# One kernel, one change: the four gating products of an adapter column block put in one row with priority

## The chip, the cores and the metric

The kernel runs on one core of one Trainium2 chip. The metric is the device time of one execution in microseconds (us); of several executions the median is used. A profile is one execution recorded by the hardware profiler; its times are counted from the first instruction of the program.

The engines have short names in the profile: PE is TensorE (matmuls; PEld its weight loads), DVE is VectorE, ACT is ScalarE, POOL is GpSimd, SP is SyncE, which here only issues DMAs. A q after the name means the engine's instruction queue.

## What is computed

Two batches of 1024 rows and 2048 columns pass through two steps, both with a layer norm in front and a residual sum behind. Cut to what matters:

```python
x = x + matmul(fake_quant(layernorm(x), s1, z1), fake_quant(ctx_4096, s2, z2))
u = layernorm(x)                       # seen as 8 groups of 256 rows
A_eff = einsum('bn,nri->bri', gate, lora_A)     # 16 adapters of rank 32, 8 groups
B_eff = einsum('bn,nor->bor', gate, lora_B)
delta = einsum('bor,btr->bto', B_eff, einsum('bri,bti->btr', A_eff, u))
delta += einsum('or,btr->bto', lora_B_shared, einsum('ri,bti->btr', lora_A_shared, u))
x = x + matmul(u, kernel) + bias + delta
```

The change concerns `A_eff` and `B_eff`: for each group the 16 adapters are summed with the group's gates as weights. The kernel does these sums on TensorE, as products with a small gate matrix.

## The kernel before

**Stages.** Each batch has a quantised stage (the first matmul, in bf16) and then a feed-forward stage (the second matmul in f32, by seven outer times seven inner products of half blocks, `product` at L813 and L829, which takes the place of eight by eight). The profile shows the quantised stage of batch 0 in the first 178 us and that of batch 1 from about 550 to 713 us.

**Pairs.** In the quantised stage the unit of work is a pair (`Pair`, L513): one block of 512 columns `n` and one group `g` of 256 rows. Its accumulator `pa` has two halves of 128 rows, one bank each. For each half, ACT first writes a starting value into the bank (`begin`, L526, which reads a row term and the column term of the block), and then 16 bf16 products of 128x128 by 128x512 are added on PE (L530). When both halves are done, DVE adds the pair to `y` (`end`, L547) and takes statistics (L551). Three accumulators go round, so that the pair after the next but one waits for `end`. `begin` is queued with priority (L558).

**Adapters.** For each of four column blocks of `lora_A` and of `lora_B`, and for each batch, `gated_sums` (L570) computes one tile `pg` of 128 rows and 512 columns: four products with the gate matrix `gmat` (128x32) as weights, each of which writes its own 32 rows of `pg`. That makes 16 calls with 64 products; an f32 product stands in the trace as two matmul records, so there are 128 records. The four inputs come in two loads of two parts; SP issues each part as a DMA (L216) into buffers named `lit`, of which there are ten. After two products the buffer of the first load is given back and the next load is traced (`load_next`, L204), then the same for the second load. `gated_copy` (L588, L591) has DVE copy `pg` into one of three buffers `q2b`, which the quantisation of the context uses in turn as well. For `lora_A` four transposes `pga` (L601) and four small copies (L607) follow; for `lora_B` eight DMAs to `bd` in device memory (L617).

**Buffers in PSUM.** `pg` comes from the pool `ps_m` under the tag `pm`, which has two buffers. The same two serve `pt` (L423, transposes of the quantised rows), `pcp` and `pc` (L486 and L505, column sums of the context block), `pga`, `ptz` (L633, transposes of the second norm) and `px` (L649).

**What sets the order.** The instructions are traced in program order, and a planner at compile time lays out each engine's queue from that trace: whenever an engine is free in the planner's own model of the run, it takes the ready instruction with the lowest priority number, which is its place in the trace. Ready means that what it depends on is done and that a buffer of its tag is free. Inside `tc.high_priority()` the numbers are those of the start of the program. On the chip each engine then works through its queue strictly in that order and waits on semaphores. The first 78 us or so and part of what follows are an exception: the steps of `entry` (L923) are chained by hand (`STEPS`, `in_order`), the calls for column blocks 0 and 1 of `lora_A` in batch 0 among them (steps g0 and g1). The other 14 calls are free: `lora_a_step` (L594, called at L1049 and L1063) and `lora_b_step` (L612, called at L1066 and L1084), all between pairs.

Of the kernel before, what the change touches and what calls it, by code (L numbers as in the profile page):

```python
# [98 lines left out]
def tile_quant_xattn_then_lora_ffn(  # L99
# [33 lines left out]
    GP = GPB * RC  # L133
# [70 lines left out]
    def load_next():  # L204
        while todo and len(loaded) < ahead[0] and todo[0][0] <= batch[0] and lit.spare:
            _, srcs = todo.popleft()
            if isinstance(srcs, int):
                load_x(0, srcs)
                continue
            buf = lit.take()  # L210
            t = flat(buf).rearrange("p (k n) -> p k n", k=2)
            if len(srcs) == 1:
                nc.sync.dma_start(out=t, in_=srcs[0])
            else:
                for c, src in enumerate(srcs):
                    nc.sync.dma_start(out=t[:, c, :], in_=src)  # L216
            loaded.append((len(srcs), buf, t))

    def next_loaded(parts):

        got = next(e for e in loaded if e[0] == parts)
        loaded.remove(got)
        return got[1:]
# [342 lines left out]
    def gated(nm):  # L566

        return gated_copy(gated_sums(nm))

    def gated_sums(nm):  # L570
        ps = ps_m.tile([P, NB], F32, tag="pm", name=f"pg_{nm}")
        for h in range(2):
            buf, t = next_loaded(2)
            for c in range(2):
                row = (2 * h + c) * GP
                nc.tensor.matmul(  # L576
                    ps[row : row + GP, :],
                    gmat.rearrange("p i a r -> p (i a r)"),
                    t[:, c, :],
                    start=True,  # L580
                    stop=True,
                    skip_group_check=True,
                )
            lit.give(buf)
            load_next()
        return ps
# [336 lines left out]
    def entry():  # L923
# [21 lines left out]
        def ad_sums(n):  # L945
            ad[n] = gated_sums(f"a0_{n}")
# [275 lines left out]
```

## Time and profile before

| | us |
|---|---|
| median of 3 runs | 1090.87 |
| the three runs | 1091.78, 1090.87, 1089.13 |
| the profiled execution, first to last instruction (its span) | 1086.6 |
| PE busy | 1063.4 (98% of the span) |
| DVE busy | 759.3 (70%) |
| ACT busy | 247.6 (23%) |
| POOL busy | 267.8 (25%) |
| DMA traffic | 261.35 MB, 241 GB/s in the mean |
| granted TensorE clock, mean | 0.994 |

The profile gives no other time of its own for the profiled execution than the span. The timed runs lie 4.3 us above it in the median, for what comes before the first and after the last instruction. A difference of about 0.3% (3.3 us) is what a measurement of this kernel can tell from none.

How to read the lines that follow in this document: a line of a timeline gives the start and the length of a run of like instructions on one engine, then the engine, the line of the code, what is written and read with the tile shape, and how many instructions there are. Brackets at the end give the idle time of the engine before it and what ended it. A run of matmuls ends when its last matmul has left the array; the next run can start before that, since matmuls overlap.

### The profile page before, as it was taken

How to read it: one execution, taken by the hardware profiler on the slowest of the kernel's cores; microseconds unless marked ns; L12 is line 12 of the kernel's file. 1: busy time of each engine (PE TensorE's matmuls, PEld its weight loads, DVE VectorE, ACT ScalarE, POOL GpSimd, SP SyncE). 2: the span in 40 equal slices, each digit the busy share in tenths (PEclk: the TensorE clock that was granted, in tenths of full speed). 3: DMA queues.
4: the chain of work that ended last, by engine and by line, in shares of the span. 5: the costliest groups of instructions: out<-in, count | busy, mean ns of one | idle time of the engine just before them, and what ended most of it. 6: DMA issues, size and time to landing. Idle time of an engine off the chain costs nothing.

```text
span 1086.6 us, 10640 instructions
## 1 busy us (share of the span) xinstructions
PE 1063.4 (98%) x3932; PEld 491.3 (45%) x3932; DVE 759.3 (70%) x941; ACT 247.6 (23%) x351; POOL 267.8 (25%) x112
## 2 busy tenths in 40 slices
PE   5999999999999999999999999999999999999998
PEld 2444445544444444444444433555444444444443
DVE  7986776756877686677858645757569677756851
ACT  5866133210000000001676631331000000000000
POOL 0000003243434314362000000034344532253500
PEclk7999999999999999999999999999999999999999
DMA  9979758876897575798682394679668874748511
GB/s 344 378 200 295 214 189 327 311 250 218 290 361 271 181 269 182 255 357 300 221 281 49 124 245 164 222 273 349 237 237 292 293 266 154 270 144 301 212 40 58
DMA packets 120380, 261.35 MB, mean 241 GB/s; under 512 B 11400, under 2 KB 15624, under 8 KB 119304
## 3 DMA queue, kind: packets, MB, share of 16 engines
q1 hardware_dynamic: 99840, 219.24, 59.1%
q10 hardware_dynamic: 20168, 40.38, 10.9%
q0 software_dynamic: 320, 1.05, 0.3%
q8 instruction: 31, 0.51, 0.2%
q14 instruction: 21, 0.17, 0.1%
HBM read 224.99 MB, written 37.75 MB: 242 GB/s over the span
## 4 chain that ended last, share of the span: by engine, by line
PE 87%; DVE 5%; DMA 4%; ACT 2%; issue 1%; SPq 0%; ACTq 0%
PE fu L829 34%; PE fv L829 17%; PE pa L530 14%; PE fw L829 9%; DMA lit<-in_ctx_dram 3%; PE pl L695 3%; PE px L649 3%; PE ptz L633 2%; DMA y<-in_x_dram 1%; PE pg_b L576 1%; DVE st L383 1%; PE pg_a L576 1%; ACT big L412 1%; PE pt L423 1%; DVE big L629 1%
## 5 line engine op out<-in xcount | busy, mean ns | idle before, releaser
L829 PE MATMUL fu<-big,lit 128*128 128x512 f32 x896 | 395.3, 593 | 0.0
L829 PEld LDWEIGHTS fu<-big,lit 128*128 128x128 f32 x896 | 168.7, 190 | 206.2 <-issue 204.9
L530 PE MATMUL pa<-big,big 128*128 128x512 bf16 x1024 | 238.8, 381 | 5.0 <-DVE big L428 2.6
L829 PE MATMUL fv<-big,lit 128*128 128x512 f32 x448 | 197.9, 594 | 0.0
L772 POOL TENSOR_TENSOR lit<-lit,lit 128x1024 f32<-128x1024 f32 x56 | 164.2, 2940 | 116.4 <-PE fw L829 49.2
L763 POOL TENSOR_TENSOR lit<-lit,lit 128x1024 f32<-128x1024 f32 x40 | 100.2, 2508 | 289.1 <-DMA lit<-zs 257.7
L772 DVE TENSOR_TENSOR big<-big,big 128x2048 f32<-128x2048 f32 x56 | 159.6, 2853 | 5.9 <-PE ptz L633 5.3
L530 PEld LDWEIGHTS <-big 128*128 128x128 bf16 x1024 | 96.7, 98 | 136.5 <-issue 31.8
L853 DVE TENSOR_TENSOR y<-y,fu 128x1024 f32<-128x1024 f32 x92 | 108.6, 1215 | 50.7 <-PE fu L829 50.5
L829 PEld LDWEIGHTS fv<-big,lit 128*128 128x128 f32 x448 | 84.3, 190 | 105.0 <-issue 104.7
L853 DVE TENSOR_TENSOR y<-y,fv 128x1024 f32<-128x1024 f32 x48 | 56.8, 1218 | 89.4 <-PE fv L829 89.4
L458 ACT ACTIVATE q2b<-lit,sc,inv 128x1024 int16<-128x1024 f32 x64 | 76.3, 1232 | 161.8 <-DMA lit<-in_ctx_dram 126.1
L763 DVE TENSOR_TENSOR big<-big,big 128x2048 f32<-128x2048 f32 x40 | 104.2, 2604 | 11.8 <-DMA big<-in_w_dram 11.8
L829 PE MATMUL fw<-big,lit 128*128 128x512 f32 x224 | 99.6, 593 | 0.0
L680 POOL DMA_DIRECT2D bp<-bd x4 | 2.7, 664 | 376.8 <-DVE rstd_z L358 183.4
L684 ACT COPY pl<-bias 128x1024 f32<-128x1024 f32 x16 | 16.3, 1018 | 294.4 <-DVE y L706 281.4
L547 DVE SCALAR_TENSOR_TENSOR y<-pa,k_s,y 128x1024 f32<-128x1024 f32 x32 | 41.0, 1280 | 47.0 <-PE pa L530 46.8
L829 PEld LDWEIGHTS fw<-big,lit 128*128 128x128 f32 x224 | 41.8, 190 | 51.4 <-issue 50.2
L853 DVE TENSOR_TENSOR y<-y,fw 128x1024 f32<-128x1024 f32 x24 | 28.4, 1216 | 50.9 <-PE fw L829 50.9
L526 ACT ACTIVATE pa<-bp,r_s 128x512 f32<-128x512 f32 x58 | 39.0, 685 | 84.8 <-PE pa L530 54.8
L383 DVE BATCH_NORM_STATS2 st<-y 128x6 f32<-128x512 f32 x64 | 41.4, 680 | 5.4 <-DMA y<-in_x_dram 5.3
L551 DVE BATCH_NORM_STATS2 st<-y 128x6 f32<-128x512 f32 x64 | 40.1, 678 | 0.1
(92 smaller groups left out, 637.3 us busy)
## 6 DMA issues: line engine op xcount, KB each, us to landing
big<-in_w_dram SPq DMA_DIRECT2D x96, 1024.0 KB
lit<-zs SPq DMA_DIRECT2D x88, 512.0 KB
lit<-in_ctx_dram SPq DMA_DIRECT2D x64, 512.0 KB
out_dram<-y ACTq DMA_DIRECT2D x30, 512.0 KB
zs<-lit ACTq DMA_DIRECT2D x24, 512.0 KB
lit<-in_lora_a_dram SPq DMA_DIRECT2D x32, 256.0 KB
lit<-in_lora_bt_dram SPq DMA_DIRECT2D x32, 256.0 KB
y<-in_x_dram SPq DMA_DIRECT2D x16, 512.0 KB
```

Source lines behind the costliest of these rows:

```text
L383: nc.vector.bn_stats(st1[:, self.m, n, :], self.y[:, ds(n * NB, NB)])
L458: nc.scalar.activation(qi, t, AF.Relu, bias=z2, scale=inv2)
L526: nc.scalar.activation(self.pa[:, j, :], colt[self.n], AF.Identity, bias=r_s[:, m : m + 1])
L530: nc.tensor.matmul(self.pa[:, j, :], self.c1T[:, k, ds(j * P, P)], self.c2[k // 8][:, k % 8, :], start=not self.begun[j], stop=(k == KT - ...
L547: return nc.vector.scalar_tensor_tensor(yp, self.pa, s12, yp, ALU.mult, ALU.add)
L551: nc.vector.bn_stats(st2[:, self.g * MG + j, self.n, :], y[self.g][:, j, ds(self.n * NB, NB)])
L649: nc.tensor.matmul(px[i * 2 * R : (i + 1) * 2 * R, :], acat[:, k, ds(3 * pr + i, 2), :].rearrange("p s r -> p (s r)"), zqs[i][k // KQ][:, ...
L695: nc.tensor.matmul(pl[j][i][:, half], axT[rows, pr, ds(j * P, P)], bt[rows, half], start=False, stop=True, skip_group_check=True,)
L763: line(eng.tensor_tensor(got[0], got[0], got[1], ALU.add if terms[1][2] > 0 else ALU.subtract))
L772: line(eng.tensor_tensor(out_t, at[p], at[q], op))
L829: nc.tensor.matmul(ps[m], at[:, k, ds(m * P, P)], bt[:, k, :], start=(opens and k == 0), stop=(ends and k == KQ - 1), skip_group_check=True,)
L853: line(nc.vector.tensor_tensor(yp, yp, whole[chain], op))
```

## The change

`gated_sums` takes both loads first. The four products are then issued in one block, inside `tc.high_priority()`, and from the last row block to the first. Both buffers are given back, and the next loads traced, after all four.

```diff
     def gated_sums(nm):
         ps = ps_m.tile([P, NB], F32, tag="pm", name=f"pg_{nm}")
-        for h in range(2):
-            buf, t = next_loaded(2)
-            for c in range(2):
-                row = (2 * h + c) * GP
+        got = [next_loaded(2) for _ in range(2)]
+        with tc.high_priority():
+            for c in (3, 2, 1, 0):
                 nc.tensor.matmul(
-                    ps[row : row + GP, :],
+                    ps[c * GP : (c + 1) * GP, :],
                     gmat.rearrange("p i a r -> p (i a r)"),
-                    t[:, c, :],
+                    got[c // 2][1][:, c % 2, :],
                     start=True,
                     stop=True,
                     skip_group_check=True,
                 )
+        for buf, _ in got:
             lit.give(buf)
             load_next()
         return ps
```

The shapes, the number of products, their inputs and the copies behind them stay as they are.

## The prediction

> **What bounds the kernel.** I read the page first, then the PE timeline around every call of the gating products, then who waits for whom.
>
> ```profile
> span 1086.6 us, 10640 instructions
> ...
> PE 1063.4 (98%) x3932; PEld 491.3 (45%) x3932; DVE 759.3 (70%) x941; ACT 247.6 (23%) x351; POOL 267.8 (25%) x112
> ...
> PE 87%; DVE 5%; DMA 4%; ACT 2%; issue 1%; SPq 0%; ACTq 0%
> ```
>
> PE is busy 98% of the span and makes 87% of the chain that ended last. In the two stretches with gating products (80 to 160 us, 605 to 695 us) PE is busy in nearly every microsecond, so PE time taken out there should reach the end, unless something else then comes late.
>
> The timeline of PE shows how the 16 calls stand now. One call is a whole row of four products (8 records), another is broken:
>
> ```profile
> 79.25 1.02 PE L530 MATMUL pa<-big,big 128*128 128x512 bf16 x4 [0.43 <-ACT pa L526]
> 80.20 1.06 PE L576 MATMUL pg_a<-lit,gmat 128*32 128x512 f32 x8
> 81.20 1.47 PE L530 MATMUL pa<-big,big 128*128 128x512 bf16 x6
> ```
>
> ```profile
> 99.74 5.13 PE L530 MATMUL pa<-big,big 128*128 128x512 bf16 x23
> 104.80 1.05 PE L576 MATMUL pg_a<-lit,gmat 128*32 128x512 f32 x2
> 105.78 3.63 PE L530 MATMUL pa<-big,big 128*128 128x512 bf16 x16
> 109.34 1.06 PE L576 MATMUL pg_a<-lit,gmat 128*32 128x512 f32 x6
> 110.33 5.86 PE L530 MATMUL pa<-big,big 128*128 128x512 bf16 x26
> ```
>
> The reader is to see that two records, six and eight all take 1.05 or 1.06 us: products that write different rows of `pg` run side by side in the array, and each group pays once, however many stand in it. Seven calls are whole (they start at 80.20, 83.03, 119.15, 128.24, 158.63, 617.04 and 693.06 us). Nine are broken into one product, then 16 products of a pair, then three (104.80, 132.79, 141.88, 608.82, 636.92, 646.44, 657.90, 666.99 and 676.07 us; the three follow 4.5 us later).
>
> **What a group costs.** Take it from the starts of its neighbours. Sixteen `pa` products take 3.63 us and the last lasts 0.38, so they follow each other at (3.63 - 0.38) / 15 = 0.216 us. The last `pa` before the lone product started at 99.74 + 5.13 - 0.38 = 104.49; the next starts at 105.78. Without the group it would have come 0.216 after the former, so the lone product costs 105.78 - 104.49 - 0.216 = 1.07 us. The three cost 110.33 - 109.03 - 0.216 = 1.08 us. The row of four costs 81.20 - 79.89 - 0.216 = 1.09 us. A broken call pays 1.07 + 1.08 = 2.15, a whole one 1.09: **1.06 us less for each of nine calls, 9.6 us in all.** That would be the answer if the place of the lone product cost nothing otherwise.
>
> **The cover that goes.** All nine lone products stand between the two halves of a pair. There PE has something to wait for:
>
> ```profile
> 616.51 0.60 PE L601 MATMUL pga<-ident,q2b 128*128 128x128 f32 x4
> 617.04 1.06 PE L576 MATMUL pg_a<-lit,gmat 128*32 128x512 f32 x8
> 618.04 1.47 PE L530 MATMUL pa<-big,big 128*128 128x512 bf16 x6
> 620.29 0.38 PE L530 MATMUL pa<-big,big 128*128 128x512 bf16 x1 [0.78 <-ACT pa L526]
> ```
>
> ```profile
> L526 ACT ACTIVATE pa<-bp,r_s x30: 670/691/692, 559.6 to 697.1; 128x512 f32<-128x512 f32 x30
> ...
> its engine sat idle before it (us, times) until:
>   PE pa L530: 32.6, 9
> ```
>
> The starting value of a second half (L526, 0.69 us) waits for the last product of the first half, though it writes another bank; ACT's idle time in that stretch ends on `pa` nine times. At 620.29 nothing filled the hole: from product to product PE needed 1.159 us in place of 0.216, so an open hand-over loses 0.94 us. The lone product covers just this hole. If all four move elsewhere, the hole needs another cover. The first products of the next pair can be it, where that pair's first half has its starting value: at 114.7, 569.5, 576.5 and 593.8 us they are, and the step across the hand-over is only 0.295 to 0.297 us, a loss of 0.08. At 631.4 us it is 0.464, a loss of 0.25.
>
> So a call whose row falls into the hand-over saves 1.06 us; a call whose row falls elsewhere saves 2.15 - 1.09 - 0.08 = 0.98 with the next pair as cover, and 2.15 - 1.09 - 0.94 = 0.12 with an open hand-over. Ends for the nine: 1.1 and 9.6 us. I take 0.98 for eight and 0.12 for one, the call at 657.90: there the next pair needs a new column term, which DVE only ends at 658.6 us (L511 begins at 657.79 and takes 0.81), so its products can't stand in. 8 x 0.98 + 0.12 = **8.0 us**. The mean loss over the six uncovered hand-overs above, 0.25 us, would give 9 x (1.06 - 0.25) = 7.3, which is close.
>
> **Where the rows go.** With priority they go when their four parts have landed and one of the two `pm` buffers is free, and before any `pa` product. Landing: DMA is saturated from 84 to 122 us (its share is 1.00 to 1.08 in most stretches of 4 us) and idle at 124 to 128, so every adapter load of batch 0 is in by about 122. The loads of `lora_B` are 16 DMAs of 256 KB issued from 104.3 to 115.2; at some 274 GB/s one takes 0.96 us; counted back from 122, my estimate is 110, 114, 118 and 122 us for the four blocks, against starts at 128.2, 132.8, 141.9 and 158.6. In batch 1 DMA stays full until about 647, and the same count gives 625 to 628 us for the block that starts at 636.9. Most rows can come earlier by several us, without a wait for data.
>
> **The other parts.** The next loads are traced after all four products, not after two. In a whole row the products start 7 ns apart, so that delay is nothing; in a broken call the second product came with the last group anyway. SP's own waits for `pg_a` are 9.5 us in three cases, all with DMA work still queued; an earlier row only shortens them. Taking both loads first needs two buffers that are already loaded: no instruction. DVE has the same 16 copies of 0.68 us, and between 104 and 120 us it is busy without a break, so an early row waits for its copy with a `pm` buffer in hand: nothing if the second buffer suffices, priced below if not. The order 3, 2, 1, 0 changes no cost, as each product writes its own rows. The feed-forward stages keep every instruction; the chains through DVE at their start (PE waits there at 184.2 and 719.1 us) begin at the end of a pair and move with it.
>
> The Trainium skill has a rule that speaks against the row: "TensorE: Matmul & The Clock Gate", Part 3, says that a weight load overlaps products in flight only when it goes to another row group. Here the four products share all rows and differ in columns. By that rule six further weight loads of 0.108 us each (the median of the trace) would stand in line, a row would cost 1.09 + 0.65 = 1.74 us, and the change would save 9 x (2.15 - 1.74) = 3.7 us before the hand-overs. The trace shows otherwise: the row of four at 80.20 has its first four weight loads 5 to 7 ns apart and costs 1.09 us.
>
> **The sum.** The span is 1086.6, and 1086.6 - 8.0 = 1078.6. The timed runs lie 4.3 us above the span, so the forecast for the median is 1090.87 - 8.0 = **1082.9 us**.
>
> **Rivals.**
> 1. The cover is missed: most hand-overs stay open, because the next pair isn't ready in the planner's order. Nine times 0.12 saves 1.1 us: 1089.8. For it: 620.29. Against it: four of six uncovered hand-overs lost only 0.08.
> 2. Rows queued before their loads land. The planner's picture of DMA time may be too short where DMA is saturated, and PE's queue is strict. The exposed blocks are the third and fourth of `lora_A` and perhaps two of `lora_B` in each batch. A row queued right after the column sums of batch 1 (about 625 us) meets data at 625 to 628, so 0 to 3 us; I take 4 us over both batches: 1086.9. Against it: now PE ends a wait on adapter data once, 0.4 us.
> 3. It doesn't do what it says: with priority the two products of the first load go as soon as they are ready, and the others later. A call then still pays twice, and whole calls break. No gain: 1090.9.
> 4. **Slower:** early rows hold the `pm` buffers. A row takes a buffer when its data are there but gives it back only after its copy, which keeps its place on DVE and needs a `q2b` buffer. In batch 1 the first block of `lora_A` is loaded by about 550 us and its copy stands at 614.8; a row that went at 550 would keep one of two buffers for 60 us. Transposes (`pt`, eight tiles from 583 to 608 us), column sums and `ptz` (32 tiles) would go through one buffer, each waiting for the copy of the one before: 0.68 us (L428) and its hand-offs, about 0.9. It decides from 8.0 / 0.9, nine such waits that nothing fills; with some 16 of them the result is 1090.9 - 8.0 + 14.4 = 1097.3. Against it: PE has products of pairs to put into most of these waits.
>
> **Chances.** The forecast (within about 2 us) 0.60; rival 2, 0.10; rival 1, 0.10; rival 3, 0.05; rival 4, 0.15. About 0.3% (3.3 us) is what a measurement of this kernel can tell from no change. Forecast and rival 2 lie below 1087.6: faster 0.70. Rivals 1 and 3: same 0.15. Rival 4: slower 0.15. The range leaves rival 4 out. Its low end is the full 9.6 us and the spread of the runs, 1.3 us: 1080.0. Its high end takes in rivals 1 to 3 with the spread: 1092.2.
>
> **What would show it.** Right: the PE timeline has 16 groups of eight records at L576, none of two or six; each costs 1.09 us by its neighbours; steps across the old hand-overs are about 0.3 us; the end of the quantised stage comes about 3 us earlier in batch 0 and 5 us in batch 1. The sum would be wrong if hand-overs at L530 show idle time that ends on ACT L526 (rival 1), if L576 waits for DMA (rival 2), if groups of two and four records appear (rival 3), or if `pt`, `ptz`, `pcp` or `pc` wait for DVE copies with `pg` in between (rival 4).

## The result, and the profile after

The changed kernel takes 1106.92 us (median of 4 runs, 1104.97 to 1107.41) against 1091.01 for the kernel before on the same chip: a ratio of 1.0164, 95% interval 1.0146 to 1.0181. It is slower: the medians are 15.9 us apart, the ratio makes it some 18 us. The forecast was 8 us faster, and the time lies above the range. (The experiments ran on other chips, where the kernel before took 1087.3 to 1088.7 us. They are compared by ratio to the kernel before on their own chip.)

First the page of the changed kernel, the same lines that were read before:

```profile
span 1105.6 us, 10625 instructions
...
PE 1062.2 (96%) x3932; PEld 493.7 (45%) x3932; DVE 757.2 (68%) x941; ACT 247.4 (22%) x351; POOL 262.1 (24%) x112
...
PE 79%; DMA 10%; DVE 7%; ACT 2%; issue 1%; SPq 0%; ACTq 0%; DVEq 0%
```

The span grew by 19.0 us, while PE busy fell by only 1.2. PE idle time (span less busy) went from 23.2 to 43.4 us. In the chain that ended last, DMA rose from 4 to 10%. So PE now waits, and more of the chain that ended last is transfers.

The rows themselves are as forecast. The PE timeline has all 16 calls whole, and two calls of a batch even stand as one group:

```profile
128.31 1.06 PE L575 MATMUL pg_b<-lit,gmat 128*32 128x512 f32 x8
129.31 0.39 PE L530 MATMUL pa<-big,big 128*128 128x512 bf16 x1
129.63 1.92 PE L575 MATMUL pg_b<-lit,gmat 128*32 128x512 f32 x16
```

The time went at the start of both feed-forward stages. The first outer product there (`fu`) is followed by `fw`, which needs the weight block b21: SP loads it in two DMAs of 1 MB (L753), and DVE adds the two (L763). In the timeline of the changed kernel, batch 0 and then batch 1:

```profile
185.76 3.60 PE L829 MATMUL fu<-big,lit 128*128 128x512 f32 x8
192.76 2.29 DVE L763 TENSOR_TENSOR big<-big,big 128x2048 f32<-128x2048 f32 x1 [7.56 <-DMA big<-in_w_dram]
195.11 6.47 PE L829 MATMUL fw<-big,lit 128*128 128x512 f32 x10 [5.75 <-DVE big L763]
...
728.54 4.45 DVE L763 TENSOR_TENSOR big<-big,big 128x2048 f32<-128x2048 f32 x1 [8.06 <-DMA big<-in_w_dram]
733.05 1.12 PE L829 MATMUL fw<-big,lit 128*128 128x512 f32 x2 [3.27 <-DVE big L763]
738.76 1.94 PE L633 MATMUL ptz<-ident,big 128*128 128x128 f32 x8 [4.59 <-DVE big L629]
```

Read the brackets from the bottom up: PE waits for DVE, DVE waits for the load. In batch 1 the norm of the next tile (L629) stands behind the late sum in DVE's queue, and there is a second wait of 4.59 us. The three waits are 13.6 us.

In batch 0 the load explains the wait: the sum takes its usual 2.29 us. In batch 1 it takes 4.45, and two small steps of the norm (L349) take 4.40 us together, where they take 0.35 in batch 0. POOL's own sums (L772) stand beside them:

```profile
728.50 2.34 POOL L772 TENSOR_TENSOR lit<-lit,lit 128x1024 f32<-128x1024 f32 x1 [9.16 <-DMA zs<-lit]
730.92 4.27 POOL L772 TENSOR_TENSOR lit<-lit,lit 128x1024 f32<-128x1024 f32 x1
733.10 4.40 DVE L349 SCALAR_TENSOR_TENSOR nt_z<-ve_z,r_z 128x1 f32<-128x1 f32 x2
735.15 2.33 POOL L772 TENSOR_TENSOR lit<-lit,lit 128x1024 f32<-128x1024 f32 x1
```

The DVE sum ends at 732.99, 2.15 us after the end of the first POOL sum; the two small steps end at 735.21 and 737.51, each 0.02 us after the end of a further one. So DVE stood still while POOL's sums ran. All 20 traces of this case agree: each of the 673 sums of weight blocks on DVE that took more than 2.32 us ended 2.14 to 2.16 us after the end of a POOL sum that it met, and each of the 20 steps at L349 that took more than 0.4 us ended 0.01 to 0.02 us after one. Of the 7.86 us of waiting in batch 1, an estimate from these durations, (4.45 - 2.29) + (4.40 - 0.35) = 6.2 us, is POOL's hold on DVE. The load is still behind it in part: POOL's sums had waited for DMA too (9.16 us for `zs`), so all came at once.

In the kernel before, PE did not wait there. But look how close it was, in its timeline (the lines of POOL are the sums that ran when b21 landed):

```profile
183.60 2.70 POOL L772 TENSOR_TENSOR lit<-lit,lit 128x1024 f32<-128x1024 f32 x1
185.13 3.60 PE L829 MATMUL fu<-big,lit 128*128 128x512 f32 x8
186.07 2.38 DVE L763 TENSOR_TENSOR big<-big,big 128x2048 f32<-128x2048 f32 x1 [1.50 <-DMA big<-in_w_dram]
188.57 4.50 PE L829 MATMUL fw<-big,lit 128*128 128x512 f32 x10
...
718.43 2.69 POOL L772 TENSOR_TENSOR lit<-lit,lit 128x1024 f32<-128x1024 f32 x1
720.54 2.74 DVE L763 TENSOR_TENSOR big<-big,big 128x2048 f32<-128x2048 f32 x1 [1.15 <-DMA big<-in_w_dram]
723.40 4.50 PE L829 MATMUL fw<-big,lit 128*128 128x512 f32 x10
```

The sum ends at 186.07 + 2.38 = 188.45, and `fw` starts at 188.57; in batch 1 it is 723.28 and 723.40. **Block b21 was ready 0.12 us ahead of its use, in both batches, and DVE had idled for its data before that.** The 0.12 itself comes from POOL, whose sums end 2.15 us ahead of those on DVE here too (186.30 and 721.13). With the usual 2.29 us the block would have been ready at 188.36 and 722.83, an estimate that leaves the load 0.2 and 0.6 us to spare. So the kernel before was bound there by PE and, within 0.6 us, by a chain through DMA as well.

A long wait is paid twice. Ten `fw` records took 4.50 us before and take 6.47 after the wait. The stretches of the changed kernel around it say why; behind the busy times stand the granted clock, the DMA share and GB/s:

```profile
185.00:190.00 5.00, 4.36 (x16) 2.10 (x15) 0.20 (x3) 1.37 (x4) 4.52 (x2) 1.00 1.00 384
190.00:195.00 5.00, 0.00 (x0) 0.00 (x0) 2.24 (x2) 0.00 (x0) 0.00 (x0) 0.72 0.65 261
195.00:200.00 5.00, 4.89 (x7) 2.21 (x8) 2.41 (x11) 0.00 (x0) 0.00 (x0) 0.60 0.72 261
```

After the idle stretch the granted clock is 0.60. The Trainium skill ("TensorE: Matmul & The Clock Gate", Part 1) says that the array falls to half its clock after about 3.4 us without work and stays there until it has been busy for as long. The trace agrees in kind, with a granted clock of 0.50 from 192.2 to 198.9 us and 6.47 us for 4.50 us of work. But the clock fell sooner, 2.8 us after PE's last matmul (189.36), and waits of 1.9 to 2.8 us brought a lower clock at times as well (last section).

The sum: idle time +20.2 us. PE busy -1.2, of which the rows take away some 8 (measured below as 8.1), so that other matmuls were busy some 7 us longer. The low clock accounts for about 5 of these, by an estimate: PE was busy for 10.1 us in the stretches with a clock of 0.50 (192.2 to 198.9, 635.9 to 639.3 and 734.9 to 741.7 us), and half of that is extra. Together 19.0.

**Why is b21 late?** Look at SP's timeline, of the kernel before and then of the changed one. The bd DMAs (L617) carry a copied `pg` to device memory, eight per call of `lora_B`; the loads at L753 are weight blocks:

```profile
126.61 2.10 SPq L753 DMA_DIRECT2D big<-in_w_dram  x2
130.25 5.24 SPq L617 DMA_DIRECT2D bd<-q2b  x8
137.43 0.93 SPq L753 DMA_DIRECT2D big<-in_w_dram  x2
```

```profile
130.24 5.07 SPq L617 DMA_DIRECT2D bd<-q2b  x8
135.41 6.44 SPq L753 DMA_DIRECT2D big<-in_w_dram  x3
141.94 1.21 SPq L617 DMA_DIRECT2D bd<-q2b  x2
...
178.98 1.67 SPq L753 DMA_DIRECT2D big<-in_w_dram  x2
```

The early row let the planner queue the eight bd DMAs of the first call ahead of the first weight loads. On the chip they wait for the copy (L591) until 130.24, so SP does nothing for 12 us and DMA is idle from 125 to 130 us (share 0.01; 0.39 before). In the kernel before, SP stood still for 10.9 us there, until a pair gave the weight block its buffer (L530, 126.6), and its first bd DMAs started at the same 130.25. The first weight block now starts 8.8 us later. Not all of that is SP's order: with the loads first (below) they start at 131.29, when a buffer comes free. The loads of b21 start at 178.98 and 179.48, where they started at 173.56 and 178.54.

### The profile page after: what moved, and what is told of

Same layout as the page of the kernel before. It is cut to its first block, busy times and chain, and to the rows that moved or that the text cites. A ratio compares the mean times of both kernels' runs of the same rounds, so it can differ in the third digit from the quotient of the medians.

```text
span 1105.6 us, 10625 instructions
## 1 busy us (share of the span) xinstructions
PE 1062.2 (96%) x3932; PEld 493.7 (45%) x3932; DVE 757.2 (68%) x941; ACT 247.4 (22%) x351; POOL 262.1 (24%) x112
## 4 chain that ended last, share of the span: by engine, by line
PE 79%; DMA 10%; DVE 7%; ACT 2%; issue 1%; SPq 0%; ACTq 0%; DVEq 0%
PE fu L829 33%; PE fv L829 17%; PE pa L530 10%; PE fw L829 9%; DMA big<-in_w_dram 4%; PE pl L695 3%; PE px L649 2%; PE ptz L633 2%; DMA y<-in_x_dram 2%; DVE st L383 1%; DMA lit<-in_lora_a_dram 1%; DMA gate_b<-in_gate_dram 1%; DVE big L763 1%; DMA lit<-in_ctx_dram 1%; DMA bd<-q2b 1%
## 5 line engine op out<-in xcount | busy, mean ns | idle before, releaser
L530 PE MATMUL pa<-big,big 128*128 128x512 bf16 x1024 | 238.1, 383 | 6.3 <-DVE big L428 2.5
L772 POOL TENSOR_TENSOR lit<-lit,lit 128x1024 f32<-128x1024 f32 x56 | 161.3, 2889 | 151.8 <-PE fw L829 77.8
L763 POOL TENSOR_TENSOR lit<-lit,lit 128x1024 f32<-128x1024 f32 x40 | 96.9, 2423 | 295.2 <-DMA lit<-zs 258.6
L772 DVE TENSOR_TENSOR big<-big,big 128x2048 f32<-128x2048 f32 x56 | 158.0, 2824 | 5.1 <-PE ptz L633 4.6
L530 PEld LDWEIGHTS <-big 128*128 128x128 bf16 x1024 | 98.0, 98 | 133.9 <-issue 26.3
L763 DVE TENSOR_TENSOR big<-big,big 128x2048 f32<-128x2048 f32 x40 | 105.7, 2642 | 27.8 <-DMA big<-in_w_dram 27.8
L829 PE MATMUL fw<-big,lit 128*128 128x512 f32 x224 | 102.1, 605 | 9.0 <-DVE big L763 9.0
L526 ACT ACTIVATE pa<-bp,r_s 128x512 f32<-128x512 f32 x58 | 39.0, 685 | 93.6 <-PE pa L530 51.4
L383 DVE BATCH_NORM_STATS2 st<-y 128x6 f32<-128x512 f32 x64 | 41.4, 680 | 6.1 <-DMA y<-in_x_dram 6.1
L633 PE MATMUL ptz<-ident,big 128*128 128x128 f32 x256 | 35.6, 283 | 7.6 <-DVE big L629 7.5
```

What stands on the lines that cost most here:

```text
L383: nc.vector.bn_stats(st1[:, self.m, n, :], self.y[:, ds(n * NB, NB)])
L526: nc.scalar.activation(self.pa[:, j, :], colt[self.n], AF.Identity, bias=r_s[:, m : m + 1])
L530: nc.tensor.matmul(self.pa[:, j, :], self.c1T[:, k, ds(j * P, P)], self.c2[k // 8][:, k % 8, :], start=not self.begun[j], stop=(k == KT - ...
L633: nc.tensor.transpose(pt[:, k, :], t[:, ds((4 * u + k) * P, P)], ident)
L763: line(eng.tensor_tensor(got[0], got[0], got[1], ALU.add if terms[1][2] > 0 else ALU.subtract))
L772: line(eng.tensor_tensor(out_t, at[p], at[q], op))
```

## The experiments

The theory after that reading was that SP's order alone does it (Theory 1, later A). Its rivals: the priority itself, through early rows that hold `pm` buffers and DVE (2); open hand-overs and waits of rows for their loads (3); the grouping (4). Later came B (stores compete with b21's loads), C (its second load starts too late) and D (the bytes that DMA has to move there).

### Without the priority, with it for lora_B alone

```diff
-        with tc.high_priority():
+        with nullcontext():
             for c in (3, 2, 1, 0):
```

> The change without its priority: both loads first, order 3, 2, 1, 0, but the products keep their place in the trace. All 16 rows still stand whole in the planned order. In the planned SP queue batch 0 has two weight loads (L753) ahead of the first eight bd DMAs (L617), as before; batch 1 has the bd DMAs ahead, as after the change. Theory 1 (bd DMAs ahead of the weight loads delay block b21, so that the feed-forward stage starts late): the feed-forward start of batch 0 comes 1 to 3 us earlier than before, that of batch 1 is late by some 10 us against the end of its quantised stage; median 1094 to 1099. Theory 2 (the priority: early rows hold pm buffers and put their copies ahead of other DVE work): no late start at all, 1081 to 1086. Theory 4 (the grouping, or the later trace place of the next loads, does the harm): about as after, 1104 to 1108.

Measured: ratio 0.999 (0.9971 to 1.0008), 1086.8 us, no change from the kernel before. Its rows are all whole, too. Theory 1 put it at 1094 or more, Theory 2 at 1086 or less with no late start, Theory 4 (the grouping) at 1104 or more: none holds. In batch 0 the weight loads stand ahead of the bd DMAs as before, and still the PE timeline has (both lines stop where the stretch shown ends, so they hold fewer than the ten records)

```profile
194.11 4.43 PE L829 MATMUL fw<-big,lit 128*128 128x512 f32 x5 [5.42 <-DVE big L763]
...
725.20 1.98 PE L829 MATMUL fw<-big,lit 128*128 128x512 f32 x4 [2.15 <-DVE big L763]
```

Batch 0 also has three open hand-overs (102.53, 108.09 and 124.56 us: 1.45, 0.63 and 0.78 us of waiting for L526), which eat what its rows save. Batch 1 shortens its quantised stage, from its first to its last `pa`, by 7.3 us against the kernel before and gives 1.7 of it back at b21.

```diff
-        with tc.high_priority():
+        with tc.high_priority() if nm[0] == "b" else nullcontext():
```

> Priority kept for the lora_B calls only; the lora_A calls are grouped without it. In the planned SP queue batch 0 has the first eight bd DMAs ahead of all weight loads, as after the change; batch 1 has two weight loads ahead, as before. Theory 1: the feed-forward start of batch 0 is late by some 8 us as after the change, that of batch 1 is not; median 1095 to 1100. Theory 2 (early lora_B rows hold pm buffers and DVE time, whatever SP does): both batches late, 1103 to 1108. Theory 3 (open hand-overs and waits of lora_A rows for their loads): only the 3 to 4 us of those waits go, 1102 to 1104.

Measured: 1.0067 (1.0049 to 1.0086), 1094.5 us. `fw` waits 6.70 us in batch 0 and 3.66 us in batch 1. The expectation had two weight loads ahead in batch 1; on the chip the bd DMAs stand ahead there too (665.23, the loads at 670.33), so this run doesn't part the theories. It shows that the priority costs time (1.0067 and 1.0164 against 0.999). That SP's order of bd DMAs and first loads is not the whole cause follows from the run without priority: 5.42 us of waiting in batch 0 with the loads ahead, and only 2.15 in batch 1 with the bd DMAs ahead (663.05, the loads at 668.14).

### The bd DMAs on another queue

```diff
-                nc.sync.dma_start(
+                nc.gpsimd.dma_start(
                     out=bd[b][i::2, i, ds(c * RC, RC), ds(n * NB, NB)],
```

> The changed kernel with the 64 bd DMAs of L617 issued by POOL, not by SP; SP's queue then has only loads in that stretch. PE's order is the same but for places near the end of the quantised stage. Theory 1: SP no longer waits for the copies of the rows, the weight loads go out by 130 us or earlier, L763 is in time, the waits of fw for block b21 (5.75 and 3.27 us, with the slow matmuls behind them) go: 1081 to 1088. Theories 2 and 3: the waits stay, since copies, pm buffers and rows stand as before: 1102 to 1107.

> Control: the kernel before with the same 64 DMAs on POOL. Theory 1: two weight loads already stand ahead of the bd DMAs before the change, so little is gained: 1087 to 1092. If the move by itself is worth as much here as in the changed kernel (10 us or more), Theory 1 is not what separates the two kernels.

Measured: after 1.0177 (1.016 to 1.0194), before 1.0221 (1.0206 to 1.0236). The edit did far more than take the DMAs from SP: the waits on b21 went, but others came, on `ptz` for L629 (5.30, 5.78 and 3.71 us in the kernel before with this edit). Why the norm comes late there was not followed up; in the wait of 5.78 us, at least, three of its steps met sums on POOL (L349 2.25, L358 2.25 and L629 3.56 us, usually 0.35, 0.28 and 1.53). As a test of Theory 1 the pair says little. It says one thing: with SP free of bd DMAs, the changed kernel is the faster one, by 5 us (1106.4 against 1111.6).

### The weight loads first on SP

`first.load("b11")` is traced ahead of `lora_b_step(b, 0)`, and the bd DMAs are chained behind the loads:

```diff
-        lora_b_step(b, 0)
...
-        first.load("b11")
+        loaded_b11 = first.load("b11")
+        with tc.issue_after(loaded_b11):
+            lora_b_step(b, 0)
...
-                first.load("b12")
+                loaded_b12 = first.load("b12")
...
-                lora_b_step(b, g + 1)
+                with tc.issue_after(loaded_b12):
+                    lora_b_step(b, g + 1)
```

> The changed kernel with one edit: the bd DMAs (L617) of the first lora_B call are queued on SP behind the two loads of the first weight block, those of the next calls behind the loads of the second block. SP's planned order is then that of the kernel before, in both batches; the rows keep their priority and stand whole. Theory A (bd DMAs ahead of the first weight loads make all later weight loads late): the waits of fw for block b21 (5.75 and 3.27 us, and the 4.59 us behind the second) go, with the slow matmuls after them: 1084 to 1092. Theory B (the last block, b21, is late because its two loads share the DMA engines with the eight zs stores of L640 at that time, whatever stood ahead of the first loads): the waits stay at 3 to 6 us in each batch: 1099 to 1106.

Measured: 1.0068 (1.0041 to 1.0095), 1097.1 us. One edit to SP's order gives back more than half of the loss (1.0164 to 1.0068), with the rows untouched. But `fw` still waits 4.33 and 3.33 us. Theory A is right in part; something else holds b21 up as well.

### Stores that compete with b21

In the run without priority, the second load of b21 is issued 0.7 us later than in the kernel before (179.22 for 178.54 us), but takes 12.5 us to land, not 7.4. At that time ACT issues four stores of 512 KB (L640, group 2, 183.7 to 187.3 us). The first attempt moved the wrong stores, those of group 3 (L640 again, issued from 197 us on):

```diff
-            nc.scalar.dma_start(out=zs[b][g][q], in_=zq[q])
+            (nc.sync if g == GPB - 1 else nc.scalar).dma_start(out=zs[b][g][q], in_=zq[q])
```

> The changed kernel with one edit: the four zs stores (L640) of the last group of each batch are issued by SP, where they stand behind the loads of b21, and not by ACT. Theory B: the loads of b21 land 7 to 9 us after their issue, where they took 13 and 14 us; the waits of fw shrink by 3 to 5 us in each batch and some of the low clock goes: 1092 to 1099. Theory A: the loads of b21 are late by their issue and by what stands ahead of them, so nothing changes: 1103 to 1108.

> The same move of the four stores, on the kernel that groups the four products without priority (1086.8 us). Theory B: its waits for b21 (5.42 and 2.15 us) shrink to under 1.5 us in all, with the low clock at 190 to 200 us: 1078 to 1082, faster than both kernels of the case. Theory A: the waits stay, 1085 to 1088.

> Control: the same move of the four stores on the kernel before. There the loads of b21 land 7.4 us after their issue, nearly all ahead of the four stores, and fw starts 0.1 to 0.2 us after the block is ready without idle time. Both theories: 1086 to 1091, no difference; more than 4 us faster would mean that the kernel before paid for this contention too.

Measured: 1.0152 (1.012 to 1.0184), 0.9981 (0.9965 to 0.9996) and 1.0013 (0.9995 to 1.003). Hardly a difference, as must be when the moved stores come after b21 has landed. Nothing follows for Theory B. Then the stores of group 2, on the kernel without priority:

```diff
-        for q in range(4):
+        for q in range(4 if g != 2 else 0):
             nc.scalar.dma_start(out=zs[b][g][q], in_=zq[q])
...
-        first.load("b21")
+        with tc.issue_after(first.load("b21")):
+            for q in range(4):
+                nc.sync.dma_start(out=zs[b][2][q], in_=zqs[2][q])
```

> The same kernel without priority, with another single edit: the four stores (L640) of group 2, issued by ACT at 183 to 187 us in batch 0 while the loads of b21 are under way, are issued by SP behind these loads. (The stores moved in the three kernels before were those of group 3, issued after b21 had landed: they could not test this.) Theory B: the second load of b21 lands 7 to 8 us after its issue, where it took 12.5 us; the waits of fw shrink by 4 us in batch 0 and 1 to 2 us in batch 1: 1079 to 1083. Theory C: gains of 0 to 2 us only, 1085 to 1088.

Measured: 1.0047 (1.0032 to 1.0062), 1093.3 us, slower. Yet Theory B's step holds: the second load now lands 7.65 us after its issue (179.60 to 187.25). The Trainium skill ("DMA: Bandwidth & Descriptors", Queues, rings and completion order) says that SP and ACT each have a ring on the same 16 DMA engines, which take from the rings in turn, packet by packet; 12.5 against 7.65 us for the same 1 MB agrees. The time was lost elsewhere, in this kernel's timeline:

```profile
187.34 3.25 DVE L764 TENSOR_TENSOR big<-big,big 128x2048 f32<-128x2048 f32 x1 [3.34 <-DMA big<-in_w_dram]
193.30 1.53 DVE L629 TENSOR_SCALAR big<-y,mv_z,rstd_z 128x1024 f32<-128x1024 f32 x2
194.26 1.94 PE L633 MATMUL ptz<-ident,big 128*128 128x128 f32 x8 [6.04 <-DVE big L629]
```

Block b21 comes in time, but the planner now has the transposes of group 3 ahead of `fw`, and their norm stands behind the sum in DVE's queue. POOL's sums stretch both, the sum to 3.25 us and the two steps at L349 to 2.23, which makes 2.8 of the 6.04 us.

### Earlier buffers for b21

```diff
+        first.load("b21")
         z3 = [big.take() for _ in range(2)]
         zqs[3] = [t[:, :, ds(h * GT, GT)] for t in z3 for h in range(2)]
-        first.load("b21")
```

> The kernel that groups the four products without priority (1086.8 us), with one edit: the two loads of b21 take the two buffers that come free first, and the tiles z3 of the last group, which are written some 15 us later, take the next two. Theory C (b21 is late because its second load starts only when the last pair gives its buffer back, at 179 us in batch 0, and then shares DMA with the stores of L640): the second load starts 3 us earlier or more, the waits of fw (5.42 and 2.15 us) shrink to under 2 us together, and the low clock behind them goes: 1078 to 1083, faster than both kernels of the case. Theory B (only the stores matter): 1084 to 1088.

> The changed kernel with its priority, the first weight loads ahead of the bd DMAs (1097.1 us) and also the early buffers for b21. Theory C: the waits of fw that were left (4.33 and 3.33 us) shrink to under 2 us together, with the low clock behind them: 1085 to 1090. Theory B: 1094 to 1098.

> Control: the early buffers for b21 in the kernel before. There fw starts within 0.2 us of the block and PE does not wait, so there is little to gain: 1086 to 1090 by both theories. Less than 1084 would mean that the kernel before was held back by b21 too.

Measured: 0.9995 (0.9977 to 1.0012), 1.0102 (1.0066 to 1.0138) and 1.0001 (0.9987 to 1.0015). No gain, but the edit didn't do what it was for: the second load still waited for the last pair and was issued at 179.29 us (179.22 without the edit). Theory C was not tested by it.

### A quarter of b21's bytes

These three kernels leave out three quarters of each load of b21; the rest of the block keeps old data. They tell of time only.

```diff
-                    nc.sync.dma_start(out=t, in_=w[ds(k0, KQ * P), ds(n0, NB)].rearrange("(k p) n -> p k n", p=P))
+                    kp = 1 if self.o == 0 and name == "b21" else KQ
+                    nc.sync.dma_start(
+                        out=t[:, :kp], in_=w[ds(k0, kp * P), ds(n0, NB)].rearrange("(k p) n -> p k n", p=P)
+                    )
```

> The changed kernel, leaving out three quarters of each of the two loads of b21 in both batches (256 KB in place of 1 MB; the rest of the block keeps old data). Nothing else is edited: the bd DMAs still stand ahead, the loads are issued when they were. Theory D (the bytes: DMA works without a break over the last 30 us of the quantised stage, so whatever comes late there lands late, and b21 is last): block b21 is there by 188 us, the waits of fw and what follows them (5.75, 3.27, 4.59 us) go, with the slow matmuls behind them: 1085 to 1091. If the waits stay above 3 us each (1098 to 1107), it is the time of issue or the place of L763 on DVE, not the bytes.

> The kernel that groups the products without priority (1086.8 us), with the same three quarters of the b21 loads left out. Theory D: its waits of 5.42 and 2.15 us go and the rows' gain is seen whole in batch 1 and against three open hand-overs in batch 0: 1077 to 1081. If it is not the bytes: 1084 to 1088.

> Control: the kernel before with the same loads cut to a quarter. PE does not wait for b21 there, it starts fw 0.1 to 0.2 us after the block is ready, so fewer bytes bring nothing: 1086 to 1090 by Theory D. If it falls below 1084, cutting these bytes brings time by itself and the two runs above must be read against it.

Measured: after 1.0041 (1.0024 to 1.0058), grouped 0.9924 (0.9896 to 0.9952), before 1.0004 (0.999 to 1.0018). Fewer bytes of b21 are worth nothing to the kernel before, 13 us to the changed one (1.0164 to 1.0041) and 7 us to the grouped one (0.999 to 0.9924). The grouped kernel's timeline, batch 0:

```profile
185.00 4.14 DVE L766 TENSOR_TENSOR big<-big,big 128x2048 f32<-128x2048 f32 x1
185.83 3.60 PE L832 MATMUL fu<-big,lit 128*128 128x512 f32 x8
189.27 4.49 PE L832 MATMUL fw<-big,lit 128*128 128x512 f32 x10
```

`fw` follows `fu` without a wait and at full clock. (The sum, with its data there in time, takes 4.14 us because it meets a POOL sum, and 4.15 in the kernel before with the same cut; it ends 0.12 us ahead of `fw` in both, as it did with the whole load.) Between the kernel before and the grouped one, both with a quarter of b21, PE busy falls from 1060.2 to 1052.1 us, by 8.1, and the time from 1089.6 to 1080.7: **this is what the rows are worth where b21 doesn't hold PE up.** One reservation: the edit also let the second load go earlier, by 3.7 us in the grouped kernel (175.56) and 1.7 in the changed one (177.77). In the changed one, the time from issue to landing fell from 13.2 to 5.8 us, so there the bytes weigh more than the issue; in the grouped one the two are not told apart. The changed kernel keeps 4 us of loss even so, and stands 12 us behind the grouped one with the same cut (1093.05 against 1080.72). So b21's bytes are not all that the priority costs. In its profile PE waits 2.33 us for the sum of b21, which takes 6.31 us because it meets two POOL sums in a row, 2.57 us with a row queued ahead of its loads (rival 2, at 627.36), 1.70 and 0.78 us for L526, and up to 1.55 us at a time for L629.

### Grouped in batch 1 only, and the norm ahead of b21

The kernel without priority gained in batch 1 and lost in batch 0. So batch 0 keeps the code of before:

```diff
+        if nm[1] == "0":
+            return gated_sums_by_halves(ps)
         got = [next_loaded(2) for _ in range(2)]
```

> No work left out: batch 0 as before the change, the four products grouped without priority in batch 1 only. In the run with both batches grouped, batch 1 gave 5.1 us back in all (late by 7.0 us when it began, by 1.9 us in its feed-forward stage) and batch 0 lost 7.6. Taken apart: 1081 to 1085, faster than both kernels of the case. If the gain of batch 1 hangs on the state that batch 0 leaves behind: 1086 to 1090.

Measured: 0.9957 (0.994 to 0.9975), 1084.0 us: faster than both kernels. `fw` starts without a wait in batch 0 and waits 3.48 us in batch 1. Then the order on DVE that the run with the moved stores had shown:

```diff
-        first.block("b21")
+        with tc.issue_after(normed[b, 3 * MG, 0].ins):
+            first.block("b21")
```

> The version with only batch 1 grouped (1084.0 us), with one more order: DVE adds block b21 only after it has normed the first tile of group 3, so that this norm (L629 and the small steps ahead of it) no longer stands behind the late b21 in DVE's queue, and PE can transpose that tile while b21 is on its way. Theory D: b21 still lands when it did; what PE has to do before it needs b21 grows by the first transposes of group 3 (1 to 3 us), so the wait of 3.48 us in batch 1 shrinks by 1 to 3 us with some of the low clock: 1079 to 1083. If DVE's order doesn't matter: 1083 to 1086.

Measured: 0.9947 (0.9926 to 0.9968), 1083.3 us, the fastest kernel that does all the work. By its ratio it can't be told from the run before it, but its waits went, as its timeline in batch 1 shows:

```profile
719.36 1.06 PE L656 MATMUL ptz<-ident,big 128*128 128x128 f32 x8 [0.28 <-DVE big L650]
720.66 1.15 PE L656 MATMUL ptz<-ident,big 128*128 128x128 f32 x8 [0.24 <-ACT big L657]
722.18 1.13 PE L852 MATMUL fw<-big,lit 128*128 128x512 f32 x2 [0.38 <-DVE big L786]
```

The second load of b21 lands at 718.24 us, 11 us after its issue, a longer way than the 7.4 us of the kernel before; PE has transposes to do meanwhile.

With the stores of group 2 behind b21's loads as well:

> The same, and the four stores of group 2 stand on SP behind the loads of b21 in both batches, which made b21 land 7.7 us after its issue where it took 12.5. Theory D with the order on DVE mended: no wait on b21 in either batch, 1077 to 1081. If moving the stores costs by itself, as in the run where it was tried alone (6.04 and 4.65 us of waits on L629, by my reading the norm behind b21 on DVE): 1084 to 1092.

Measured: 1.0022 (1.0003 to 1.0041), 1091.0 us: the gain is gone, in waits of 3.77 and 3.79 us of `ptz` for the norm. The norm is ahead of b21 in DVE's queue here, so that order is not why moving these stores costs time. In batch 0 two small steps of that norm (L349) take 1.39 and 2.37 us where they take 1.09 and 0.21 in the run above; they end at 186.10 and 188.39, each 0.02 us after the end of a POOL sum. In batch 1 it is 3.71 us for the two. Against the usual 0.35 that is 3.4 us in each batch, most of both waits: moving the stores costs time here because the norm then meets POOL's sums. Why they meet was not followed up.

## Why the prediction was wrong

**The failed step** is in "The other parts": "The feed-forward stages keep every instruction; the chains through DVE at their start (PE waits there at 184.2 and 719.1 us) begin at the end of a pair and move with it." One chain there doesn't begin at a pair. The sum of b21 on DVE begins when a load lands, and that hangs on SP's queue and, as argued below, on DMA's throughput over the last 30 us of the stage. In the changed kernel PE waited 5.75 and 3.27 us for that sum, and 4.59 us for the norm behind it. I looked at the two waits of 0.5 and 0.8 us that the trace named, and not at the operand without a wait that came 0.12 us ahead of its use, nor at POOL's sums, which hold DVE at the same place. PE time taken out of the stage therefore had no path to the end without that load.

**What was left out** is the other half. I counted the 16 copies behind the rows, but not the eight bd DMAs behind each `lora_B` copy, nor that they share SP's strict queue with the weight loads. Moved ahead of the first loads, they cost about 10 us of the 18 (the run with the weight loads first: ratio 1.0164 to 1.0068).

**Point by point.** 
- Sixteen whole rows, each at one group's price: right. The rows are worth 8.1 us of PE busy and 8 to 9 us of time where b21 is no limit; the sum said 8.0. That it came so close is partly luck: in that kernel PE waited 2.2 us more for L526 than in the kernel before (3.4 for 1.2), where the sum allowed 1.6 for all hand-overs.
- The cover of the hand-overs: right in the changed kernel, with one newly open hand-over (1.28 us at 110.12). In the kernel without priority rival 1 came true in batch 0, with three.
- Rival 2 came true once, at its place: the row after the column sums of batch 1 waited 2.77 us for its data at 634.52.
- Rival 3 did not happen. Rival 4 was the one with the right sign, but not by its mechanism: no `pt`, `ptz`, `pcp` or `pc` waits with `pg` in between. Its 1097.3 was still too low.
- The end of the quantised stage was to come 3 and 5 us earlier. In batch 0 it came 1 us later (last `pa` at 179.45 for 178.50). In batch 1 it took 8.7 us less (its first `pa` is 8.4 us late, at 563.09 for 554.70, and its last ends 0.3 us early). There the gain was made, and was lost at the next step.
- PE time taken out "should reach the end, unless something else then comes late": something did, and the chance of 0.15 for slower was too small for a kernel in which DMA's share is 0.9 in the stretch that the change shortens (0.89 from 160 to 192 us).

**Shown and not shown.** Shown: the waits on b21, the low clock behind them, the 10 us of SP's order, POOL's hold on DVE, the worth of the rows without b21. Argued only: that DMA's throughput delays b21 in every kernel with whole rows; the quarter runs fit, but in one of them the time of issue moved as well. Open: how the 12 us between the changed and the grouped kernel with a quarter of b21 divide among the waits listed there, and how much of the loss would go if POOL's sums stood elsewhere; no run moved them.

## What to carry to other kernels

An engine that is busy 98% and never waits may still have a second chain nearly as long beside it: before you price time taken out of an engine, measure for the next stage's operands how long they are ready before their first use, above all those that a DMA brings. Where an instruction takes much longer than its like, look what another engine ran at that moment. When a step moves earlier, follow everything behind it to the last DMA, and look what else stands in that strict queue: a small transfer that waits for its data holds up the large loads behind it. Group the work without priority first, and only where the transfers have room.

## What the runs showed of the hardware

- A wait of PE of about 2 us or more often brings a low granted clock afterwards, but not by a sharp bound: 1.89, 2.07 and 2.77 us did (0.83 in the 10 us around them), 2.15, 2.36 and 2.69 us did not, and waits of 5.1 to 6.7 us on b21 gave 0.66 each time.
- One load of 1 MB took 7.4 to 13.2 us from issue to landing at the same place in the program. With four stores of 512 KB on another queue beside it, it took 12.5 us, and 7.65 with these stores behind it.
- The sum of two 1 MB blocks on DVE (L763) took 2.29 us as a rule, and 2.33 to 6.31 us where it met a POOL sum that had begun before it: it then ended 2.15 us after that POOL sum, or after the second of two in a row (6.31 us). DVE steps of 128x1 elements (L349, 0.1 to 0.2 us each) were held up to 2.38 us in the same way, and POOL's sums took 4.3 to 4.4 us, not 2.3, when they met one on DVE.
- Eight DMAs of 32 KB (16 rows of 2 KB each), queued on SP, held it for 5 to 13 us. Much of that is waiting for earlier DMAs: in the kernel before, 14.1 us behind weight loads and 11.9 us behind stores, over all 64 of them.
